# A graph kernel: the GRU state as one operation over both halves, LeakyReLU on ScalarE, and other times in the scheduler's account

## Chip, cores and metric

The kernel runs on one core of a Trainium2 chip. The metric is the device time of one execution in microseconds. The kernel before takes 2144.81 us (median of 3 runs, 2143.91 to 2145.84).

## What is computed

The input is 128 graphs of 128 nodes with 256 features (x), and an adjacency matrix per graph. Two residual layers follow each other, each after a layer norm and a ReLU. All is float32.

```
def _gru_cell(inp, h, w_ih, w_hh, b_ih, b_hh):
    gi = inp @ w_ih.T + b_ih
    gh = h @ w_hh.T + b_hh
    i_r, i_z, i_n = jnp.split(gi, 3, axis=-1)
    h_r, h_z, h_n = jnp.split(gh, 3, axis=-1)
    r = jax.nn.sigmoid(i_r + h_r)
    z = jax.nn.sigmoid(i_z + h_z)
    n = jnp.tanh(i_n + r * h_n)
    return (1.0 - z) * n + z * h
...
for i in range(L):
    m = jnp.einsum('bnd,de->bne', h, weight[i])
    aggr = jnp.einsum('bst,bsd->btd', A, m)
    h = _gru_cell(aggr, h, w_ih, w_hh, b_ih, b_hh)
...
Wh = jnp.einsum('bnf,of->bno', h, W)
s1 = Wh @ a1
s2 = Wh @ a2
e = jax.nn.leaky_relu(s1[:, :, None] + s2[:, None, :], negative_slope=ALPHA)
e = jnp.where(mask, -jnp.inf, e)
att = jax.nn.softmax(e, axis=-1)
att = jnp.where(mask, 0.0, att)
return jnp.einsum('bij,bjo->bio', att, Wh)
```

## The kernel before

**Tiles.** Four graphs make a group (G = 4), so there are 32 groups. The state of a group is held in columns: features on partitions, the 512 nodes of the group on the free axis, in two halves of 128 features (`hT`, 128x2x512). The gathering over neighbours needs it in rows (`h`, nodes on partitions).

**One GRU step** (`gru_step`, from L662) makes the gate products of a group. Two blocks of seven products each follow one another. A product is three matmuls of 128x256, into one of the PSUM banks c1_0, c1_1, c2, u and m7; Strassen-like sums save one product of eight (`moving_sums`, L447; `stationary_sums`). In each block the order is: u, m7, u again, c1_0, u again, c2, c1_1. Bank u is used three times. After its second product VectorE must compute c2 = u + m (L711) before TensorE can go on in u; that addition lies beside the product of c1_0. After its third, ScalarE copies u to c1_1 (L716), and VectorE computes c22 = u + m (L720), before the next block begins in u. ScalarE evaluates the gates (L738, L745, L773). Sigmoids are written as tanh, so factors 0.5 appear.

**Candidate and state.** `candidate` (L625) multiplies the reset gate into the hidden part, one operation for each half (L629). `state` (L633), once for each half, applies Tanh on ScalarE (L637) and then three VectorE operations (L639, L641, L645).

**Between steps.** Before the next step of a group the new state is brought into rows: by TensorE when the next step of the group comes two slots later (`rows`), else by 32x32 block transposes on VectorE and two trips of four DMAs through DRAM (`to_rows_by_blocks`, L537; L546). `prologue` normalises a new group and makes its columns: by TensorE (`to_columns`, L455; L462, copies L472) for the first four groups, by blocks and DRAM (`to_columns_by_blocks`, L514; L523) for later ones.

**Second layer** (`epilogue`, L860). The state goes back to rows; x is loaded again (`load_x1`, two buffers) and added (L886, L884 in the last three groups); then norm, ReLU (L435), two score products per graph (L903), the second score spread over partitions by a DRAM line (in the last three groups by TensorE, L913); then the score sum on ScalarE (L939), LeakyReLU on VectorE (L946), mask (L950, L952), row maximum (L958), Exp (L962), a transpose (L566 and DRAM, or TensorE L971 with the copy L975), the two products pq (L593) and po (L1003), the residual (L1010), and the store.

**What sets the order.** Steps of several groups are interleaved: a plan sorts the steps (g, l) by 3g + 4l, so that the steps of one group lie two to four slots apart. Every instruction is put in program order by a scheduler within the kernel (class `Order`, L171). Side work is written as generators. Each `yield (engine, length, ready, room)` names an engine, a length in us, the time from which it can start, and perhaps a buffer to wait for. `fill` puts such work behind the products, engine by engine, as the reckoned clock has room; an engine named in `close` must be clear again when the product ends. The numbers in the yields are the account; they cost no time on the chip, but they decide the order of each queue. LAND = 2.5 is the account's time for a DMA to land, HOP = 0.2 for a handover. All DMAs are issued from one queue, SP, in this order.

Of the kernel before, what the change touches and what calls it, by code (L numbers as in the profile page):

```python
# [8 lines left out]
F32 = mybir.dt.float32  # L9
# [8 lines left out]
G = 4  # L18
# [9 lines left out]
def preln_gnn_kernel(  # L28
# [30 lines left out]
    def dma(dst, src):  # L59
        put(nc.sync.dma_start(dst, src))  # L60
# [110 lines left out]
    class Order:  # L171
        def __init__(self):
            self.free = dict.fromkeys((PE, ACT, DVE, POOL, SP, "port"), 0.0)
            self.tasks = []

            self.rooms = {"misc": [0.0] * 3, "tq": [0.0] * 2, "h": [0.0] * ROWS, "x1": [0.0] * 2, "prT": [0.0] * 2}
            self.next, self.room_of = dict.fromkeys(self.rooms, 0), {}

        def begin(self, engine, ready, room=None, count=1):
# [20 lines left out]
        def open(self, room, name):  # L200
            self.room_of[name] = room, self.next[room]
            self.next[room] = (self.next[room] + 1) % len(self.rooms[room])
            if room == "misc":
                return ps_misc.tile([P, T], F32, tag="misc", name=name)
            if room == "h":
                return work.tile([P, G, D], F32, tag="h", name=name, bufs=ROWS)
            if room == "prT":
                return work.tile([P, G, P], F32, tag="prT", name=name)
            if room == "x1":
                return io.tile([P, G, D], F32, tag="x1", name=name, bufs=2)  # L210
            return work.tile([P, C, T], F32, tag=room, name=name)
# [214 lines left out]
        put(nc.gpsimd.tensor_tensor(nb[:, all_], nb[:, all_], rstd[:, all_], ALU.mult))  # L426
        return rstd, nb, t

    def norm_apply(src, graphs, rstd, nb, ready, name, h=None):

        for k in graphs:
            t = yield (ACT, 0.5, ready, "h") if h is None else (ACT, 0.5, ready)
            if h is None:
                h = order.open("h", f"h_{name}")
            put(nc.scalar.activation(  # L435
                h[:, k, :], src[:, k, :], AF.Relu, bias=nb[:, k : k + 1], scale=rstd[:, k : k + 1]
            ))
        return h, t
# [183 lines left out]
    def state_rows(s):  # L622
        s.h, s.h_ready = yield from to_rows_by_blocks(s.hT, s.hT_ready, f"{s.g}_{s.l}")

    def candidate(s, r, v, ready):  # L625

        for o in (1, 0):
            s.v_ready[o] = yield DVE2, 0.62, ready[o]
            put(nc.vector.scalar_tensor_tensor(  # L629
                v[:, o, :], r[:, o, :], 1.0, v[:, o, :], ALU.add, ALU.mult  # L630
            ))

    def state(s, o, old, new, v, z, ready):  # L633

        n = v[:, o, :]
        t = yield ACT, 0.66, ready
        put(nc.scalar.activation(n, n, AF.Tanh, bias=bih[:, 2 * C + o : 2 * C + o + 1], scale=1.0))  # L637
        t = yield DVE2, 0.62, t
        put(nc.vector.tensor_tensor(new[:, o, :], old[:, o, :], n, ALU.subtract))  # L639
        t = yield DVE2, 0.62, t - HOP  # L640
        put(nc.vector.scalar_tensor_tensor(  # L641
            new[:, o, :], z[:, o, :], 1.0, new[:, o, :], ALU.add, ALU.mult
        ))
        t = yield DVE2, 0.62, t - HOP
        put(nc.vector.scalar_tensor_tensor(new[:, o, :], new[:, o, :], 0.5, n, ALU.mult, ALU.add))  # L645
        s.halves.append(t)
        if len(s.halves) == C:
            s.hT, s.aT = new, None
            s.l += 1
            if s.l < NL:  # L650
                s.hT_ready = max(s.halves)
                if s.by_blocks():
                    s.rows = order.add(1, state_rows(s))
                if s.due:
                    s.task = order.add(0, inputs(s, s.hT_ready))
            else:

                pairs = range(G // 2)
                for p in [pairs] if s.g < NG - 1 else [pairs[:1], pairs[1:]]:
                    order.add(2, epilogue(s, p, max(s.halves)))  # L660

    def gru_step(s, last):  # L662
# [94 lines left out]
        reset(0, high, c1[1][:, 0, :], done)  # L757
        banks["c1_1"] = state_half(0, high, c1[1][:, 1, :], done)
        t1 = state_half(1, high, c22[:, 1, :], t22)
        s.v_ready = [0.0, 0.0]  # L760
        half_task = order.add(0, candidate(s, r, v, (banks["c1_1"], t1)))


        phase = blocks(1, [(1, (hid, given)), (2, (given,))])
# [11 lines left out]
            return t  # L776

        def add_half(o, cols, src, ready):
            t = order.take(DVE, 0.38, max(ready, s.v_ready[o]))
            put(nc.vector.tensor_tensor(v[:, o, cols], v[:, o, cols], src, ALU.add))  # L780
            return t

# [17 lines left out]
    class Group:  # L800


        def __init__(self, g):
            self.g, self.l, self.entered, self.aT = g, 0, False, None
            (self.xt, _), (self.at, self.at_ready) = xts.pop(g), ats.pop(g)
            self.scales = scales.pop(g)
            self.prT = None
            self.due = False

        def by_blocks(self):  # L810
# [2 lines left out]

    def load_x1(s):

        s.x1_ready = LAND + 1.5 + (yield SP, 0.45, 0.0, "x1")
        s.x1 = order.open("x1", f"x1_{s.g}")
        dma(s.x1, x[s.g * G : (s.g + 1) * G].rearrange("b t d -> t b d"))

# [18 lines left out]
    def prologue(s):  # L838

        g = s.g  # L840
        s.h = None
        parts = s.scales if g == 0 else [s.scales]
        for i, (rstd, nb, t) in enumerate(parts):
            n = G // len(parts)
            graphs = range(i * n, i * n + n)
            s.h, t = yield from norm_apply(s.xt, graphs, rstd, nb, t, f"a{g}", s.h)
        s.h_ready = t
        if g + XT < NG:
            order.add(1, load_task(load_rows, xts, g + XT, t))
        t2 = yield DVE, 0.36, s.at_ready  # L850
        s.A = work.tile([P, G, P], F32, tag="A", name=f"A_{g}", bufs=6)
        put(nc.vector.tensor_scalar(s.A, s.at, 0.0, None, ALU.not_equal))
        if g + AT < NG:
            order.add(1, load_task(load_adjacency, ats, g + AT, t2))
        transposed = to_columns if g < 4 else to_columns_by_blocks
        s.hT, s.hT_ready = yield from transposed(s.h, t, f"a{g}")
        if s.entered:
            s.task = order.add(0, inputs(s, s.hT_ready))

    def epilogue(s, pairs, ready):  # L860

# [6 lines left out]
        bank_t, row_t, graph_t = 0.57 * n / G + 0.02, 0.62 * n / G + 0.02, 0.11 * n  # L868

        late, h = g >= NG - 3, None  # L870
        if late:
            banks, ready = yield from to_rows(s.hT, ready, f"{name}_o", pairs)
        else:
            h, ready = yield from to_rows_by_blocks(s.hT, ready, f"b{name}")
            if g < NG - XT:
                yield from load_x1(s)
                ready = max(ready, s.x1_ready)
# [7 lines left out]
            else:  # L885
                put(nc.vector.tensor_add(x1[:, k2, :], x1[:, k2, :], h[:, k2, :]))  # L886
        rstd, nb, t = yield from norm_scales(x1, graphs, t - HOP, f"b{name}")
        h, t = yield from norm_apply(x1, graphs, rstd, nb, t, f"b{name}", h)

        v = small.tile([P, 2, G], F32, tag="s", name=f"s_{name}")  # L890
        one, two = v[:, 0, :], v[:, 1, :] if late else score_tiles[g % 2][:, 0:G]
# [13 lines left out]
                    accum_out=(one, two)[i][:, k : k + 1],  # L905
                ))

        e = None
        if late:
            t = yield PE, graph_t, t, "misc"  # L910
            p2 = order.open("misc", f"ps2_{name}")
# [4 lines left out]
        else:  # L916
# [5 lines left out]
            for q in range(Q):  # L922
# [2 lines left out]
                    line = dram.tile([G, P], F32, tag="line", name=f"line_{name}")  # L925
                part_q = slice(q * 32, (q + 1) * 32)
                dma(line[:, part_q], turned[q * 32 : q * 32 + G, :])
            t = yield SP, 0.45, t + LAND
            e = work.tile([P, G, P], F32, tag="e", name=f"e_{name}")
            dma(e, line.rearrange("(o k) p -> o k p", o=1).to_broadcast([P, G, P]))  # L930
            t = t + 2.5
            t = t + LAND
        ready = t
        for k in graphs:
            t = yield ACT, 0.4, ready
            if e is None:
                e = work.tile([P, G, P], F32, tag="e", name=f"e_{name}")
            src = p2[:, k * P : (k + 1) * P] if late else e[:, k, :]
            put(nc.scalar.activation(  # L939
                e[:, k, :], src, AF.Identity, bias=one[:, k : k + 1], scale=1.0  # L940
            ))
        if late:
            order.close(f"ps2_{name}", t)
        le = e[:, part, :]
        t = yield DVE2, row_t, t
        put(nc.vector.scalar_tensor_tensor(le, le, ALPHA, le, ALU.mult, ALU.max))  # L946

        off_ready = yield DVE, 0.36 * n / G, ready
        off = s.A[:, part, :]
# [35 lines left out]
        ))  # L985

        banks, ready = yield from gathered(h, prT, t, f"pq_{name}", graphs)
        order.close(f"h_b{name}", ready)
        hs = None
        for c, pq in enumerate(banks):  # L990
            t = yield ACT, bank_t, ready
            order.close(f"pq_{name}_{c}", t)
            if hs is None:
                hs = work.tile([P, C, T], F32, tag="hs", name=f"hs_{name}")
            put(nc.scalar.copy(hs[:, c, cols], pq[:, cols]))
        ready = t
        for half in pairs:
            t = yield PE, 1.73, ready, "misc"
            po = order.open("misc", f"po_{g}_{half}").rearrange("p (k d) -> p k d", d=D)
            for j in range(2):  # L1000
                k = half * 2 + j
                for c in range(C):
                    put(nc.tensor.matmul(  # L1003
                        po[:, j, :], hs[:, c, k * P : (k + 1) * P], gwt[:, c, :],
                        start=(c == 0), stop=(c == C - 1),
                    ))
            for j in range(2):
                k = half * 2 + j
                t2 = yield DVE, 0.4, t
# [5 lines left out]
        ks = slice(g * G + part.start, g * G + part.stop)  # L1015
        dma(out[ks].rearrange("b t d -> t b d"), x1[:, part, :])
        if g < NG - XT:
            order.close(f"x1_{g}", t + LAND)

# [135 lines left out]
```

## Time and profile before

| what | us |
|---|---|
| median of the runs | 2144.81 |
| the profiled execution | 2144.55 |
| its span | 2142.7 |
| TensorE busy | 2118.7 |
| VectorE busy | 1782.2 |
| ScalarE busy | 1295.0 |
| GpSimd busy | 119.1 |
| state operations L639, L641, L645 (VectorE) | 395.6 |
| candidate L629 (VectorE) | 123.4 |
| LeakyReLU L946 (VectorE) | 21.5 |
| score sum L939 (ScalarE) | 41.3 |

The span runs from the first to the last instruction of the profiled execution, and the execution is 1.9 us longer. In the lists, PE is TensorE, PEld its weight loads, DVE is VectorE, ACT ScalarE, POOL GpSimd, and SPq the queue that issues DMAs. A busy time is a sum over the whole span; most of it lies beside other engines' work. A group's line reads: source line, engine, operation, written tile <- read tiles, count, busy time, mean ns of one. A timeline line begins with start and duration; in brackets stands how long the engine had been idle before it, and what ended that. A line of waits reads: who <- for whom: us in total, how many times, the longest. TensorE's float32 matmuls appear as two passes each. Matmuls are pipelined, so that a listed duration is longer than the distance from one to the next.

### The profile page before, as it was taken

The page shows a single profiled execution, that of the slowest core. Times are in us where ns is not written, and L with a number is a line of the kernel's source. Part 1 is how long each engine was busy: PE and PEld are TensorE (multiplying, and loading weights), DVE is VectorE, ACT ScalarE, POOL GpSimd, SP SyncE. Part 2 cuts the span into 40 slices and gives each one's busy share as a digit, 9 for nine tenths or more (in the row PEclk, how much of TensorE's full clock was granted, in tenths as well). Part 3 has the DMA queues.
Part 4 walks back from the last instruction along what each step waited for, and adds up shares of the span by engine and source line. Part 5 has one row for each costly group of instructions (what it writes and reads, how often), then busy time and mean ns, then how long its engine had stood idle before and what let it go on. Part 6 is the DMA issues. An engine that isn't in the chain of part 4 may idle for free.

```text
span 2142.7 us, 32496 instructions
## 1 busy us (share of the span) xinstructions
PE 2118.7 (99%) x10779; PEld 1882.7 (88%) x10779; DVE 1782.2 (83%) x4176; ACT 1295.0 (60%) x2859; POOL 119.1 (6%) x204
## 2 busy tenths in 40 slices
PE   8999999999999999999999999999999999999997
PEld 7888888888888888888888888888888888888886
DVE  7778888888888888888888888888888888888776
ACT  5556656565566666656655565656656566565664
POOL 1000000000000000000000000000000000000000
PEclk9999999999999999999999999999999999999998
DMA  4144353535454255553535545354542544443301
GB/s 138 39 90 89 75 122 84 124 68 130 109 117 115 59 125 109 119 113 73 125 84 127 120 88 124 70 127 105 119 113 64 120 109 109 95 90 82 84 25 40
DMA packets 659240, 209.85 MB, mean 98 GB/s; under 512 B 569856, under 2 KB 636160, under 8 KB 659072
## 3 DMA queue, kind: packets, MB, share of 16 engines
q1 hardware_dynamic: 659072, 207.77, 43.3%
q8 instruction: 85, 1.39, 0.3%
q14 instruction: 83, 0.68, 0.1%
HBM read 120.86 MB, written 86.83 MB: 97 GB/s over the span
## 4 chain that ended last, share of the span: by engine, by line
PE 97%; DVE 2%; DMA 1%; issue 0%; SPq 0%; ACT 0%; DVEq 0%
PE c L685 34%; PE u L685 34%; PE m L685 11%; PE pa L593 8%; PE po L1003 5%; PE pq L593 3%; PE pw L356 1%; DMA x<-in_x 0%; PE pt_a L462 0%; DMA wih<-in_w_ih_t 0%; DVE prT L903 0%; DVE hT L639 0%; DMA out<-x 0%; DVE hT L641 0%; DVE c L711 0%
## 5 line engine op out<-in xcount | busy, mean ns | idle before, releaser
L773 ACT ACTIVATE z<-c,brz 128x256 f32<-128x256 f32 x384 | 185.1, 482 | 303.5 <-PE c L685 139.2
L685 PE MATMUL u<-t_h,s_hh 128*128 128x256 f32 x1152 | 343.0, 379 | 3.8 <-DVE c L711 3.8
L685 PE MATMUL c<-aT,s_f 128*128 128x256 f32 x1152 | 311.3, 379 | 0.0
L685 PE MATMUL u<-t_a,s_f 128*128 128x256 f32 x1152 | 311.3, 379 | 0.0
L738 ACT ACTIVATE r<-c,brz 128x256 f32<-128x256 f32 x384 | 174.3, 477 | 218.3 <-PE c L685 113.8
L780 DVE TENSOR_TENSOR v<-v,c 128x256 f32<-128x256 f32 x384 | 155.1, 418 | 132.1 <-ACT z L773 72.3
L685 PEld LDWEIGHTS u<-t_h,s_hh 128*128 128x128 f32 x1152 | 218.1, 190 | 34.7 <-DVE c L711 5.0
L685 PEld LDWEIGHTS u<-t_a,s_f 128*128 128x128 f32 x1152 | 218.9, 190 | 29.8
L685 PEld LDWEIGHTS c<-aT,s_f 128*128 128x128 f32 x1152 | 218.9, 190 | 29.8
L685 PE MATMUL c<-hT,s_hh 128*128 128x256 f32 x768 | 228.5, 379 | 0.0
L716 ACT COPY c<-u 128x512 f32<-128x512 f32 x192 | 109.5, 570 | 143.2 <-PE u L685 142.5
L711 DVE TENSOR_TENSOR c<-u,m 128x512 f32<-128x512 f32 x192 | 134.2, 699 | 72.4 <-PE u L685 70.4
L708 ACT COPY m<-m 128x512 f32<-128x512 f32 x192 | 112.6, 586 | 101.7 <-PE m L685 99.3
L745 ACT ACTIVATE v<-c,bhn 128x256 f32<-128x256 f32 x384 | 173.1, 481 | 0.0
L720 DVE TENSOR_TENSOR c<-u,m 128x512 f32<-128x512 f32 x192 | 131.5, 685 | 49.2 <-ACT c L716 49.2
L685 PE MATMUL m<-t_h,s_hh 128*128 128x256 f32 x576 | 171.5, 379 | 0.0
L685 PE MATMUL c<-t_h,s_hh 128*128 128x256 f32 x576 | 171.3, 379 | 0.0
L685 PEld LDWEIGHTS c<-hT,s_hh 128*128 128x128 f32 x768 | 144.8, 190 | 19.1
L685 PE MATMUL c<-t_a,s_f 128*128 128x256 f32 x576 | 155.7, 379 | 0.0
L685 PE MATMUL m<-t_a,s_f 128*128 128x256 f32 x576 | 155.6, 379 | 0.0
L685 PE MATMUL u<-aT,s_f 128*128 128x256 f32 x576 | 155.6, 379 | 0.0
L629 DVE SCALAR_TENSOR_TENSOR v<-r,v 128x512 f32<-128x512 f32 x192 | 123.4, 684 | 30.3 <-ACT v L745 28.8
(126 smaller groups left out, 3971.5 us busy)
## 6 DMA issues: line engine op xcount, KB each, us to landing
z<-tq SPq DMA_DIRECT2D x248, 128.0 KB
h<-z SPq DMA_DIRECT2D x248, 128.0 KB
xt<-in_x SPq DMA_DIRECT2D x31, 512.0 KB
z_b<-tq_b SPq DMA_DIRECT2D x116, 128.0 KB
h_b<-z_b SPq DMA_DIRECT2D x116, 128.0 KB
x<-in_x SPq DMA_DIRECT2D x29, 512.0 KB
out<-x SPq DMA_DIRECT2D x29, 512.0 KB
z_a<-tq_a SPq DMA_DIRECT2D x112, 128.0 KB
```

The costliest lines, as they stand in the source:

```text
L593: put(nc.tensor.matmul(pa[:, k * P : (k + 1) * P], h[:, k, c * P : (c + 1) * P], A[:, k, :], start=True, stop=True,))
L629: put(nc.vector.scalar_tensor_tensor(v[:, o, :], r[:, o, :], 1.0, v[:, o, :], ALU.add, ALU.mult))
L685: put(nc.tensor.matmul(to(q), S[0][:, gate_no, weight, :], moving, start=first and q == 0 and i == 0, stop=(i == len(ends) - 1), skip_grou ...
L708: put(nc.scalar.copy(m, m7))
L711: put(nc.vector.tensor_tensor(c2, u, m, ALU.add))
L716: put(nc.scalar.copy(c1[1], u))
L720: put(nc.vector.tensor_tensor(c22, u, m, ALU.add))
L738: put(nc.scalar.activation(r[:, o, cols], src, AF.Tanh, bias=brz[:, o : o + 1], scale=0.5))
L745: put(nc.scalar.activation(v[:, o, cols], src, AF.Identity, bias=bhn[:, o : o + 1], scale=0.5))
L773: put(nc.scalar.activation(z[:, o, cols], src, AF.Tanh, bias=brz[:, C + o : C + o + 1], scale=0.5))
L780: put(nc.vector.tensor_tensor(v[:, o, cols], v[:, o, cols], src, ALU.add))
L1003: put(nc.tensor.matmul(po[:, j, :], hs[:, c, k * P : (k + 1) * P], gwt[:, c, :], start=(c == 0), stop=(c == C - 1),))
```

## The change

- `candidate` and the three operations of `state` work on both halves at once (128x1024 instead of two of 128x512). They start when both halves are there. Their length in the account is 1.22 instead of 0.62.
- LeakyReLU goes from a VectorE operation of its own into the ScalarE activation that adds the first score (Prelu with alpha instead of Identity).
- The account's landing time of the x load of the second layer is 5.0 instead of 4.0, that of its store 4.5 instead of 2.5.
- The buffers of e and hs become rooms of the account. The late groups take tiles of other pools for e, hs and the normalised rows. The two parts of the last group share e, hs and the rows.
- Columns come from TensorE for the first two groups only (g < 2), not the first four.

```diff
-            self.rooms = {"misc": [0.0] * 3, "tq": [0.0] * 2, "h": [0.0] * ROWS, "x1": [0.0] * 2, "prT": [0.0] * 2}
+            self.rooms = {room: [0.0] * 2 for room in ("tq", "x1", "prT", "e", "hs")}
+            self.rooms |= {"misc": [0.0] * 3, "h": [0.0] * ROWS}
...
+    def flat(tile_):
+        return tile_.rearrange("p c t -> p (c t)")
+
     def candidate(s, r, v, ready):
 
-        for o in (1, 0):
-            s.v_ready[o] = yield DVE2, 0.62, ready[o]
-            put(nc.vector.scalar_tensor_tensor(
-                v[:, o, :], r[:, o, :], 1.0, v[:, o, :], ALU.add, ALU.mult
-            ))
+        t = s.v_ready = yield DVE2, 1.22, ready
+        put(nc.vector.scalar_tensor_tensor(flat(v), flat(r), 1.0, flat(v), ALU.add, ALU.mult))
 
     def state(s, o, old, new, v, z, ready):
 
         n = v[:, o, :]
         t = yield ACT, 0.66, ready
         put(nc.scalar.activation(n, n, AF.Tanh, bias=bih[:, 2 * C + o : 2 * C + o + 1], scale=1.0))
-        t = yield DVE2, 0.62, t
-        put(nc.vector.tensor_tensor(new[:, o, :], old[:, o, :], n, ALU.subtract))
-        t = yield DVE2, 0.62, t - HOP
-        put(nc.vector.scalar_tensor_tensor(
-            new[:, o, :], z[:, o, :], 1.0, new[:, o, :], ALU.add, ALU.mult
-        ))
-        t = yield DVE2, 0.62, t - HOP
-        put(nc.vector.scalar_tensor_tensor(new[:, o, :], new[:, o, :], 0.5, n, ALU.mult, ALU.add))
         s.halves.append(t)
         if len(s.halves) == C:
+            n, new_, z_ = flat(v), flat(new), flat(z)
+            t = yield DVE2, 1.22, max(s.halves)
+            put(nc.vector.tensor_tensor(new_, flat(old), n, ALU.subtract))
+            t = yield DVE2, 1.22, t - HOP
+            put(nc.vector.scalar_tensor_tensor(new_, z_, 1.0, new_, ALU.add, ALU.mult))
+            t = yield DVE2, 1.22, t - HOP
+            put(nc.vector.scalar_tensor_tensor(new_, new_, 0.5, n, ALU.mult, ALU.add))
+            s.halves.append(t)
             s.hT, s.aT = new, None
...
-        half_task = order.add(0, candidate(s, r, v, (banks["c1_1"], t1)))
+        half_task = order.add(0, candidate(s, r, v, max(banks["c1_1"], t1)))
...
-        s.x1_ready = LAND + 1.5 + (yield SP, 0.45, 0.0, "x1")
+        s.x1_ready = 5.0 + (yield SP, 0.45, 0.0, "x1")
...
-        transposed = to_columns if g < 4 else to_columns_by_blocks
+        transposed = to_columns if g < 2 else to_columns_by_blocks
...
+        end = g >= NG - 2
+        e_room, hs_room = (None, None) if end else ("e", "hs")
...
-        h, t = yield from norm_apply(x1, graphs, rstd, nb, t, f"b{name}", h)
+        h, t = yield from norm_apply(
+            x1, graphs, rstd, nb, t, f"b{name}", s.kept, "tq" if end else "h"
+        )
...
-            t = yield SP, 0.45, t + LAND
-            e = work.tile([P, G, P], F32, tag="e", name=f"e_{name}")
-            dma(e, line.rearrange("(o k) p -> o k p", o=1).to_broadcast([P, G, P]))
+            t = yield SP, 0.45, t + LAND, "e"
+            s.e = order.open("e", f"e_{g}")
+            dma(s.e, line.rearrange("(o k) p -> o k p", o=1).to_broadcast([P, G, P]))
...
             put(nc.scalar.activation(
-                e[:, k, :], src, AF.Identity, bias=one[:, k : k + 1], scale=1.0
+                e[:, k, :], src, AF.Prelu, bias=one[:, k : k + 1], scale=1.0, alpha=ALPHA
             ))
...
-        t = yield DVE2, row_t, t
-        put(nc.vector.scalar_tensor_tensor(le, le, ALPHA, le, ALU.mult, ALU.max))
...
         if g < NG - XT:
-            order.close(f"x1_{g}", t + LAND)
+            order.close(f"x1_{g}", t + 4.5)
```

More of the change, by code (lines that the diff above doesn't have):

```diff
@@ L206, in open @@
                 return work.tile([P, G, D], F32, tag="h", name=name, bufs=ROWS)
-            if room == "prT":
-                return work.tile([P, G, P], F32, tag="prT", name=name)
+            if room in ("prT", "e"):
+                return work.tile([P, G, P], F32, tag=room, name=name)
             if room == "x1":
@@ L427, in norm_scales, with norm_apply @@
         return rstd, nb, t
-    def norm_apply(src, graphs, rstd, nb, ready, name, h=None):
+    def norm_apply(src, graphs, rstd, nb, ready, name, kept, room="h"):
         for k in graphs:
-            t = yield (ACT, 0.5, ready, "h") if h is None else (ACT, 0.5, ready)
-            if h is None:
-                h = order.open("h", f"h_{name}")
+            t = yield (ACT, 0.5, ready) if kept else (ACT, 0.5, ready, room)
+            if not kept:
+                h = order.open(room, f"h_{name}")
+                if room == "tq":
+                    h = h.rearrange("p c t -> p (c t)").rearrange("p (k d) -> p k d", d=D)
+                kept.append(h)
+            h = kept[0]
             put(nc.scalar.activation(
@@ L759, in gru_step @@
         t1 = state_half(1, high, c22[:, 1, :], t22)
-        s.v_ready = [0.0, 0.0]
-        half_task = order.add(0, candidate(s, r, v, (banks["c1_1"], t1)))
+        s.v_ready = 0.0
+        half_task = order.add(0, candidate(s, r, v, max(banks["c1_1"], t1)))
         phase = blocks(1, [(1, (hid, given)), (2, (given,))])
@@ L778, in add_half @@
         def add_half(o, cols, src, ready):
-            t = order.take(DVE, 0.38, max(ready, s.v_ready[o]))
+            t = order.take(DVE, 0.38, max(ready, s.v_ready))
             put(nc.vector.tensor_tensor(v[:, o, cols], v[:, o, cols], src, ALU.add))
@@ L806, in __init__ @@
             self.scales = scales.pop(g)
-            self.prT = None
+            self.kept, self.prT = [], None
+            self.e = self.hs = None
             self.due = False
@@ L840, in prologue @@
         g = s.g
-        s.h = None
+        kept = []
         parts = s.scales if g == 0 else [s.scales]
@@ L845, in prologue @@
             graphs = range(i * n, i * n + n)
-            s.h, t = yield from norm_apply(s.xt, graphs, rstd, nb, t, f"a{g}", s.h)
+            s.h, t = yield from norm_apply(s.xt, graphs, rstd, nb, t, f"a{g}", kept)
         s.h_ready = t
@@ L858, in prologue, with place_of_e @@
             s.task = order.add(0, inputs(s, s.hT_ready))
+    def place_of_e(g):
+        if g < NG - 2:
+            return order.open("e", f"e_{g}")
+        return work.tile([P, 4, H], F32, tag="th", name=f"e_{g}")[:, 0:2, :].rearrange(
+            "p n t -> p (n t)"
+        ).rearrange("p (k s) -> p k s", s=P)
     def epilogue(s, pairs, ready):
@@ L874, in epilogue @@
             h, ready = yield from to_rows_by_blocks(s.hT, ready, f"b{name}")
+            s.kept.append(h)
             if g < NG - XT:
@@ L906, in epilogue @@
                 ))
-        e = None
         if late:
@@ L934, in epilogue @@
         for k in graphs:
-            t = yield ACT, 0.4, ready
-            if e is None:
-                e = work.tile([P, G, P], F32, tag="e", name=f"e_{name}")
+            t = yield (ACT, 0.4, ready, e_room) if s.e is None else (ACT, 0.4, ready)
+            if s.e is None:
+                s.e = place_of_e(g)
+            e = s.e
             src = p2[:, k * P : (k + 1) * P] if late else e[:, k, :]
             put(nc.scalar.activation(
-                e[:, k, :], src, AF.Identity, bias=one[:, k : k + 1], scale=1.0
+                e[:, k, :], src, AF.Prelu, bias=one[:, k : k + 1], scale=1.0, alpha=ALPHA
             ))
@@ L987, in epilogue @@
         banks, ready = yield from gathered(h, prT, t, f"pq_{name}", graphs)
-        order.close(f"h_b{name}", ready)
-        hs = None
+        final = pairs[-1] + 1 == G // 2
+        if final:
+            order.close(f"h_b{g}_0", ready)
+        if final and not end:
+            order.close(f"e_{g}", ready)
         for c, pq in enumerate(banks):
-            t = yield ACT, bank_t, ready
+            t = yield (ACT, bank_t, ready, hs_room) if s.hs is None else (ACT, bank_t, ready)
             order.close(f"pq_{name}_{c}", t)
-            if hs is None:
-                hs = work.tile([P, C, T], F32, tag="hs", name=f"hs_{name}")
+            if s.hs is None and end:
+                hs = work.tile([P, 4, H], F32, tag="ta", name=f"hs_{g}")
+                s.hs = hs.rearrange("p n t -> p (n t)").rearrange("p (c t) -> p c t", c=C)
+            elif s.hs is None:
+                s.hs = order.open("hs", f"hs_{g}")
+            hs = s.hs
             put(nc.scalar.copy(hs[:, c, cols], pq[:, cols]))
@@ L1006, in epilogue @@
                     ))
+            if final and half == pairs[-1] and not end:
+                order.close(f"hs_{g}", t)
             for j in range(2):
```

## The prediction, made before the changed kernel had run

> **What bounds the kernel now.** I read the page first (busy shares, slices, chain of waits), then the waits of TensorE, the timeline around each, and last the end of the span.
>
> ```profile
> span 2142.7 us, 32496 instructions
> ...
> PE 2118.7 (99%) x10779; PEld 1882.7 (88%) x10779; DVE 1782.2 (83%) x4176; ACT 1295.0 (60%) x2859; POOL 119.1 (6%) x204
> ...
> PE 97%; DVE 2%; DMA 1%; issue 0%; SPq 0%; ACT 0%; DVEq 0%
> ```
>
> TensorE bounds the span. From 6.55 us to the end of its last GRU product at 2103.60 it issues one pass of 128x256 every 0.216 us with hardly a gap. So a shorter VectorE or ScalarE operation is worth nothing in itself. Time can come from four places only: fewer passes, the few places where TensorE waits, the last 36 us, and new waits. The waits of TensorE:
>
> ```profile
> PE ps L913 <- DVE prT L903: 5.6, 1, 5.6
> PE pw L356 <- DMA wih<-in_w_ih_t: 3.9, 1, 3.9
> PE u L685 <- DVE c L711: 3.8, 3, 2.5
> PE pq L593 <- ACT prT L975: 3.3, 3, 2.2
> PE po L1003 <- DVE xt L1010: 1.5, 1, 1.5
> ```
>
> The second is the start and isn't touched. The third is two stalls of 2.50 and 1.04 us at 1821.92 and 1868.30 (0.30 more at 23.72). The others lie behind 2103.60. The larger stall in the timeline:
>
> ```profile
> 1812.42 1.26 SPq L60 DMA_DIRECT2D x<-in_x  x1
> ...
> 1817.31 1.29 DVE L886 TENSOR_TENSOR x<-x,h_b 128x512 f32<-128x512 f32 x2 [2.81 <-DMA x<-in_x]
> ...
> 1821.17 0.69 DVE L711 TENSOR_TENSOR c<-u,m 128x512 f32<-128x512 f32 x1
> ...
> 1821.92 0.70 PE L685 MATMUL u<-t_h,s_hh 128*128 128x256 f32 x2 [2.50 <-DVE c L711]
> ```
>
> The residual add stood in VectorE's queue before its x had landed (4.9 us after the issue; the order reckons 4.0). L711, which frees bank u, stood behind it, and TensorE behind that.
>
> **Part by part.** The profiled execution took 2144.55 us, its span 2142.7; the median of the runs is 2144.81, 0.26 above. I sum against 2144.55.
>
> 1. Columns of groups 2 and 3 through DRAM instead of TensorE (the bound is now g < 2):
>
> ```profile
> 40.30 1.04 PE L462 MATMUL pt_a<-ident,h_a 128*128 128x128 f32 x8
> 41.17 1.03 PE L356 MATMUL pw<-wih,wt 128*128 128x256 f32 x4
> ```
>
> Eight transposes hold the stream from 40.30 to 41.17, 0.87 us; two groups, -1.7. Added: four block transposes on VectorE (0.694 each, L523), 16 DMAs on SP's queue; gone: four copies (0.583) on ScalarE. Cover: group 2 enters in the fourth step, at about 87 us, group 3 at about 150. Counting the matmuls between the block transposes and the first use in the changed order gives over 39 us, against 21.3 in the tightest place where the kernel does this now without a wait. SP's queue has room there: before the first state rows (about 70 us) it holds only loads. Without cover the loss would be some 12 us once. I take 0.
>
> 2. One operation over both halves. L645 takes 691 ns for 512 elements, L780 takes 418 for 256: 1.06 ns an element, so 1024 cost 0.691 + 512 x 0.00106 = 1.23 us. Eight operations of 0.68 to 0.69 a step (5.5 us) become four (4.9): 0.55 x 96 = 53 us less on VectorE, plus LeakyReLU (L946, 20.6 + 0.9), minus 2.8: 1782 to about 1710. Worth on the path: 0, as long as TensorE is fed. What it could cost: L711 has only about 0.4 us of room (released by the product of u, it takes 0.70, and the product of c1 beside it takes 1.30). A 1.23-us operation in front of it can be late by more than one of 0.69. I added up VectorE's work between each two such additions, in both orders, against TensorE's work between them. The tightest interval now is 9.83 us of work in 9.07 of TensorE (isolated durations; followers overlap by about 0.08), it recurs 12 times and stalls nowhere. The tightest in the changed order is 11.28 in 10.85. The order also now reckons 1.22 for what I put at 1.23, where it had 0.62 for 0.69. So 0 to +1 us; I take 0.3. Delay of the state to its second half is covered: its row form is needed three slots (65 us) later.
>
> A rule speaks against longer operations. "SBUF — State Buffer", SBUF: two separate sides, says that a VectorE operation with two SBUF inputs and a GpSimd operation that reads SBUF take one port pair as an exclusive lock for the whole instruction. By it GpSimd's three-step norm could wait 0.54 longer at each step, 1.6 us a norm. The rows do show GpSimd swinging: L422 takes 1192 ns for norm_b and 1036 for norm_a. But ScalarE waited for that norm only 1.6 us (h_a) and 0.8 us (h_b) in the whole steady part, and in the end the norms of the last group fall behind the last wide operation. By rule or row: 0 on the path.
>
> 3. Leaky ReLU inside the first score's activation (ScalarE). No row shows that function; Identity at the same line takes 402 ns (L939), and the built order still has one table load. Bounds: 0 to +0.2 us an instruction; below nothing I exclude, since the instruction count stays. ScalarE is 60% busy; only in the end would this lie on the path, 8 instructions, +1 us at most. I take 0.
>
> 4. Longer times in the order's account, rooms for e and hs. In the two stalls the residual add follows the last L1010 of the group whose buffer it reuses by about 10 us (10.4 and 9.6, counted from the order); elsewhere now 13.2 or more, without a wait. In the changed order the shortest is 19.4. Both stalls go: -3.5. What is next late: the return of e to TensorE (11.5 us after its block transpose against 10.1 now), and the score to its activation (9.0 against 11.2, where the trip line-to-e takes about 5), the rows of one late group (10.1 against 10.8), the transposes of group 30 (0.2 us of room). I put +0.3 for these.
>
> 5. The end. Seen now: from 2103.60 to the end of the last L1010 at 2139.46, 35.9 us, VectorE's chain first, then TensorE's. A wait of 5.57 us there cools TensorE:
>
> ```profile
> 2105.00:2115.00 10.00, 7.28 (x44) 6.06 (x44) 9.31 (x32) 2.86 (x6) 0.00 (x0) 1.00 0.00 0
> 2115.00:2120.00 5.00, 0.00 (x0) 0.00 (x0) 4.78 (x12) 2.47 (x7) 3.07 (x6) 0.76 0.30 105
> 2120.00:2124.00 4.00, 2.76 (x8) 1.49 (x9) 3.65 (x20) 3.50 (x13) 0.00 (x0) 0.50 0.02 6
> ```
>
> (the column before the last two is the clock). In the changed order, from the last GRU product as 0, with the rows' durations: both Tanh end at 2.3; VectorE fills this time with four score products of group 30, then three state operations to 6.15 (now: six, to 4.55, no score product yet); four more score products to 8.4; the residual add of group 31 from 9.2; statistics to 11.35; softmax work of group 30, its LeakyReLU gone, reduce at 14.05; its Exp to 15.7; pq of 30 to 18.25; po to 22.4; pq of the first half of 31 to 24.2; first score of the second half from ScalarE at 25.3; mask, reduce to 26.4; Exp to 27.3; transpose, copy, pq to 29.1; po to 31.55; L1036 to 32.5. That is 3.4 less than 35.9: 0.69 + 0.43 + 0.43 are the LeakyReLUs, the rest is the fill during Tanh and a shorter cold stretch. The four transposes of e for group 29 (0.44) stand behind the last product instead of before it, in time that TensorE waits anyway: another -0.4.
>
> A rule decides 0.8 us of it. "TensorE: Matmul & The Clock Gate", Part 1, gives half rate after an idle window of about 3.4 us. The trace agrees at 5.57 us (0.50; pq takes 3.78 against 1.95 warm) and stays at 1.00 after a gap of 2.16. In the changed order TensorE has only 0.4 us of work in the first 4.6 us. By the rule it is cold and the residual add starts at 9.2, by the row of 2.16 at 8.4. I take the rule's; by the row the end is -4.2.
>
> Sum: -1.7 - 3.5 - 0.4 - 3.4 + 0.3 + 0.3 = -8.4; 2144.55 - 8.4 = 2136.1, and with the 0.26, 2136.4 us, 0.39% faster.
>
> **Rivals.**
> - A wait takes the place of the one removed: one place in the recurring pattern (nine steps, 195 us, some 10 times) where e or a wide operation is late by 0.5 us, 10 x 0.5 = +5, 2141.4. For it: the tight room of L711. Against: every such distance that I counted is as long as one without a wait now, or nearly. 0.14.
> - Slower: wide operations that start just before bank u is released. One costs at most 1.23 - 0.4 = 0.8 us of TensorE. From 16 collisions the whole 12.7 (8.4 to lose, 4.3 to be seen as slower) is gone, so from two places in the recurring pattern: 20 x 0.85 = 17, 2153. Against: the order holds VectorE clear before that addition. 0.04.
> - The loads still come late, since SP's queue was the cause and not the account: 2136.4 + 3.5 = 2139.9. Against: the distances of 19.4 and more. 0.10.
> - The change doesn't do what it says in the end, the serial chain gains nothing: 2136.4 + 3.8 = 2140.2. 0.10, half of it within 0.2%.
> - Forecast case: 0.62, 2133.5 to 2139.
>
> **How the numbers follow.** A measurement of this kernel can tell about 0.2%, 4.3 us, from no change. Faster: 0.62 + 0.10 + 0.05 + some of the first rival's milder forms (0.04) = 0.81; slower 0.04; same 0.15. The range goes down to 2132.5 (a warm end -0.8, both +0.3 at nothing, 2 us of my hand-made end) and up to 2141.5, the first rival.
>
> **What would show it.** Right: no wait of u for L716, the new L711, beyond 0.3 us; pt_a rows x16 instead of x32; the last GRU product ends near 2098; from there to the last L1036 about 32.5 us; wide rows at 1.2 us x96; VectorE near 1710. Wrong: a u wait that recurs about every 195 us; x<-in_x still as a releaser of the residual add; wide operations well over 1.3 us.

## The result, and the profile after

| kernel | median us | against before, 95% interval | span of the profiled execution | its time |
|---|---|---|---|---|
| before | 2144.89 (20 runs beside the other) | 1 | 2142.7 | 2144.55 |
| changed | 2141.83 (2139.42 to 2143.65, 20 runs) | 0.9985 [0.9979, 0.9992] | 2139.5 | 2141.27 |

The change makes the kernel 3.1 us (0.15%) faster. The forecast was 2136.4, so more than half of the expected gain is missing; 2141.83 lies 0.3 above the range, and 0.15% is inside the 0.2% that the forecast took as no change. The first rival, a wait that takes the place of the one removed, stood at 2141.4. One of the 20 runs of the kernel before took 2471.66 us, the others 2143.57 to 2146.26; the median hardly feels it.

The page of the changed kernel says nearly what it said before; no share tells that a gain is missing.

```profile
span 2139.5 us, 32119 instructions
...
PE 2120.0 (99%) x10763; PEld 1881.6 (88%) x10763; DVE 1724.7 (81%) x3763; ACT 1301.8 (61%) x2855; POOL 104.8 (5%) x204
...
PE 96%; DMA 1%; DVE 1%; SPq 1%; ACT 1%; issue 0%; DVEq 0%; ACTq 0%
```

The list of TensorE's waits of the changed kernel tells more (waiting tile <- what it waited for: us in total, times, longest):

```profile
PE pp L988 <- ACT e L979: 3.9, 3, 2.7
PE pw L357 <- DMA wih<-in_w_ih_t: 3.8, 1, 3.8
PE pq L598 <- DMA e<-z_e: 3.1, 3, 1.6
PE pq L598 <- ACT prT L992: 2.3, 4, 0.7
...
PE u L690 <- DVE c L716: 0.3, 1, 0.3
```

The stalls of bank u are down from 3.8 us to the 0.3 at the start. The third line is new: three times in the middle of the stream, pq (the product that reads e) waits for the second leg of e's trip through DRAM: four DMAs write e there (z_e<-prT, the first leg), four bring it back (e<-z_e, the second).

The wide operations and the Prelu cost what the sum reckoned (groups by form of the changed kernel: count, busy us, mean ns, idle time ahead and its releaser):

```profile
L636 DVE SCALAR_TENSOR_TENSOR v<-r,v 128x1024 f32<-128x1024 f32 x96 | 117.4, 1223 | 20.2 <-ACT v L750 18.4
L649 DVE SCALAR_TENSOR_TENSOR hT<-z,hT 128x1024 f32<-128x1024 f32 x96 | 117.0, 1219 | 0.6
...
L958 ACT ACTIVATE e<-e,s 128x128 f32<-128x128 f32 x116 | 39.6, 399 | 0.0
L903 DVE TENSOR_TENSOR x<-x,h_b 128x512 f32<-128x512 f32 x58 | 38.4, 678 | 0.1
```

1.22 us against the 1.23 reckoned; 399 ns against 402 for Identity. The residual add L903 no longer has a load as its releaser. VectorE fell by 57.5 us (the forecast had about 72), of which nothing shows in the time.

**Where the 3.2 us of the two spans come from.** I split each profiled span at the first gate product and at the end of the last one. "Work" is the counted TensorE work in between, each form at the spacing that it has where nothing waits; "lost" is the stream minus this work. About 1.6 remain in streams without any listed wait in their middle (5.41 - 3.84 in before, 1.56 and 1.68 in two runs below). "End" runs from the last gate product to the last residual.

| us | start | stream | work | lost | end |
|---|---|---|---|---|---|
| before | 15.22 | 2088.38 | 2082.97 | 5.41 | 35.86 |
| changed | 14.22 | 2087.41 | 2080.81 | 6.60 | 34.61 |
| difference | -1.00 | -0.97 | -2.16 | +1.19 | -1.25 |

The two stalls account for -3.54 of "lost", so something new took 4.7. A second count finds the same. The changed order repeats itself every nine steps, and e makes three trips in that time. The first of the three starts with its block transpose at 259.75, 456.79, 651.79 and so on up to 1824.11 us; the distances are 197.04, 195.00, 196.50, 194.97, 195.28, 195.08, 195.51, 194.98. The undisturbed distance is 194.97, so the excess is 4.6 us.

### The profile page after: what moved, and what is told of

It reads as the page before. It is cut to its first block, busy times and chain, and to the rows that moved or that the text cites. A ratio compares the mean times of both kernels' runs of the same rounds, so it can differ in the third digit from the quotient of the medians.

```text
span 2139.5 us, 32119 instructions
## 1 busy us (share of the span) xinstructions
PE 2120.0 (99%) x10763; PEld 1881.6 (88%) x10763; DVE 1724.7 (81%) x3763; ACT 1301.8 (61%) x2855; POOL 104.8 (5%) x204
## 4 chain that ended last, share of the span: by engine, by line
PE 96%; DMA 1%; DVE 1%; SPq 1%; ACT 1%; issue 0%; DVEq 0%; ACTq 0%
PE c L690 35%; PE u L690 34%; PE m L690 11%; PE pa L598 8%; PE po L1027 5%; PE pq L598 3%; PE pw L357 1%; SPq L60 1%; DMA z_e<-prT 0%; DMA e<-z_e 0%; DMA wih<-in_w_ih_t 0%; ACT e L979 0%; DVE t_h L458 0%; PE pr_o L489 0%; ACT v L642 0%
## 5 line engine op out<-in xcount | busy, mean ns | idle before, releaser
L716 DVE TENSOR_TENSOR c<-u,m 128x512 f32<-128x512 f32 x192 | 134.1, 698 | 144.5 <-PE u L690 144.4
L721 ACT COPY c<-u 128x512 f32<-128x512 f32 x192 | 109.5, 570 | 117.8 <-PE u L690 117.5
L710 ACT COPY c<-u 128x512 f32<-128x512 f32 x192 | 109.5, 570 | 52.7 <-PE u L690 52.6
```

The lines of the kernel that those rows point to most:

```text
L710: put(nc.scalar.copy(c1[0], u))
L716: put(nc.vector.tensor_tensor(c2, u, m, ALU.add))
L721: put(nc.scalar.copy(c1[1], u))
```

## Why e came late

This is the tightest trip of e in the kernel before (timeline of before; start and duration, then engine, line and tile):

```profile
343.99 0.70 DVE L566 STREAM_TRANSPOSE prT<-e 128x512 f32<-128x512 f32 x1
344.71 2.56 SPq L60 DMA_DIRECT2D z_e<-prT  x4
349.02 1.70 SPq L60 DMA_DIRECT2D e<-z_e  x4
350.76 1.81 SPq L60 DMA_DIRECT2D h<-z  x4
354.76 1.95 PE L593 MATMUL pq<-e,h_b 128*128 128x128 f32 x16
```

SP's queue issues the first leg 0.03 us after the transpose has ended. The next entry, the second leg, stands alone behind it, and the load of the state rows comes after both. pq follows 10.8 us after the transpose began, without a wait. The same trip in the changed kernel, one of eight like it:

```profile
371.66 3.75 SPq L60 DMA_DIRECT2D z<-tq  x4
...
377.27 0.70 DVE L571 STREAM_TRANSPOSE prT<-e 128x512 f32<-128x512 f32 x1
378.93 2.83 SPq L60 DMA_DIRECT2D h<-z  x4
...
381.80 2.80 SPq L60 DMA_DIRECT2D z_e<-prT  x4
384.67 0.60 SPq L60 DMA_DIRECT2D x<-in_x  x1
386.28 1.70 SPq L60 DMA_DIRECT2D e<-z_e  x4
...
390.11 2.02 PE L598 MATMUL pq<-e,h_b 128*128 128x128 f32 x16 [1.64 <-DMA e<-z_e]
```

Here the four loads of state rows stand ahead of the first leg. They can't be issued before their z has landed, 3.5 us after the last issue of z at 375.41 (the account reckons 2.5), and the queue issues in order. So the first leg starts 3.83 us after the transpose instead of 0.03. Then x, 512 KB, goes out between the legs. The second leg takes 2.13 us from its last issue to pq. TensorE was ready for e 11.0 us after the start of the transpose, as in the undisturbed trips, and had it at 12.8.

In the eight trips of this kind the first leg starts 1.5 to 3.8 us late, and pq 12.84, 11.04, 12.49, 11.04, 11.25, 11.04, 11.08 and 11.36 us after the start of the transpose. Against 11.04 that is 3.8 us in all, of the 4.6 in the count by periods. The list of waits shows 3.1: a wait shorter than about 0.16 us, by which the listed durations of pipelined matmuls overlap, leaves no gap.

My theory after this: e's trip is late for what stands in SP's queue ahead of its legs. Two entries are suspected: x between the legs (theory A in the texts below) and the rows h ahead of the first leg (B, later B2). The rivals were wide operations that delay L716, columns or ScalarE as new causes, and the end (C; D is its clock).

## Experiments

Ratios are against the kernel before on the same chip, with the 95% interval. "Lost" and "end" are taken as above from one profiled execution each; two executions of one program differ by over 1 us in span (the changed kernel once more, below).

**The account alone.**

```diff
-        s.x1_ready = LAND + 1.5 + (yield SP, 0.45, 0.0, "x1")
+        s.x1_ready = 5.0 + (yield SP, 0.45, 0.0, "x1")
...
-            order.close(f"x1_{g}", t + LAND)
+            order.close(f"x1_{g}", t + 4.5)
```

These two lines, put into the kernel before. 

> The kernel before with nothing but the longer times of load (5.0) and store (4.5) of x in the account. If they alone take the two stalls away: TensorE's wait of u for VectorE falls from 3.8 to 0.3 us, and the time is 3.5 lower, about 2141.3. If the lighter VectorE was needed: a wait of 1 us or more stays.

Measured: 2141.01, 0.9980 [0.9973, 0.9988]. Lost 1.56 instead of 5.41, end 36.10. Its waits of TensorE:

```profile
PE ps L913 <- DVE prT L903: 5.6, 1, 5.6
...
PE u L685 <- DVE c L711: 0.3, 1, 0.3
```

Two numbers cure both stalls and give as much as the whole change. The end is as before, so nothing else is in it.

**The same two lines taken back in the changed kernel.** 

> The changed kernel with the old times of load (4.0) and store (2.5) of x in the account. If the longer times are what took the two stalls of 2.5 and 1.0 us away: a wait of u for VectorE's addition comes back, 1 us or more in total. If the lighter VectorE or the other pattern did it: no such wait. Theory A says that e's wait depends on where x stands in SP's queue, so that it changes too; time 2138 to 2145.

Measured: 2156.7, 1.0054 [1.0042, 1.0066], slower than before. Here x is issued ahead of the first leg as well. e is late in seven listed places (11.7 us) and u at two (2.3). Without its account the rest of the change costs about 11 us.

**Columns alone** (`g < 4` to `g < 2` in the kernel before). 

> The kernel before with columns from TensorE for two groups instead of four, nothing else. Prediction's part 1: sixteen transposes less, 1.7 us lower (2143.1), no wait for the columns.

Measured: 2144.24, 0.9998 [0.9990, 1.0007]. The work between is 2081.24, 1.73 less than before, as reckoned. But lost is 5.94 and the end 36.18: the stalls of bank u stay (2.7 us), and one for the first sums (L333, 0.8) is new. The time doesn't tell it from before.

**LeakyReLU on ScalarE alone**, in the kernel before:

```diff
-                e[:, k, :], src, AF.Identity, bias=one[:, k : k + 1], scale=1.0
+                e[:, k, :], src, AF.Prelu, bias=one[:, k : k + 1], scale=1.0, alpha=ALPHA
...
-        t = yield DVE2, row_t, t
-        put(nc.vector.scalar_tensor_tensor(le, le, ALPHA, le, ALU.mult, ALU.max))
```

> The kernel before with LeakyReLU in ScalarE's first-score activation and no VectorE operation for it, nothing else. The activation costs as much as before (400 ns). On TensorE's stream 0; in the end up to 1.5 us less (0.69 + 0.43 + 0.43). Its order differs, so the two stalls of 3.5 us may go too: 2140 to 2145.

Measured: 2141.41, 0.9983 [0.9976, 0.9989]. Lost 1.82: with one yield fewer the order is another one, e's trip recurs every 65 us with 12.3 us from transpose to pq, and the stalls are gone though the account of x is the old one. The end falls to 31.26, while the work before it grows to 2088.20. So this gain isn't shown to be the operation's own; it comes with another order.

**The changed kernel with candidate and state on halves again.** 

> The changed kernel with candidate and state on halves again. If wide operations cost TensorE nothing, as its trace suggests (0.3 us of wait behind VectorE's addition), the time in the steady part is the same but for e's place in SP's queue, which is another here (12.1 us to e's return instead of 11.5): e's wait goes, 2138 to 2141. If the wide operations are what made the pattern longer and the change slow: 3 us or more lower than the changed kernel, with no wait for e.

Measured: 2140.95, 0.9980 [0.9972, 0.9988]. Lost 3.50, end 32.02, no wait for e (0.8 us of what is lost is a wait for the first sums; the work before the end grows to 2086.47 in this order). The trip has the 65-us pattern of the LeakyReLU run, h is ahead of the first leg by 1.0 to 2.3 us here too, but TensorE comes 12.3 us after the transpose. So without the wide operations the kernel isn't slower, and the tight nine-step pattern comes with them. Why the scheduler falls into it isn't shown; the wide operations alone in the kernel before were not tried.

**x behind e's second leg**, in the changed kernel (`order.close(f"x1_{g}", t + 4.5)` becomes `t + 11.5`; only SP's order differs). 

> The changed kernel; the only difference is that in the recurring pattern the load of x for the second layer stands behind the four DMAs that bring e back, not between the two legs of e's trip (the account's time for the store of x is 11.5 instead of 4.5; the order of TensorE, VectorE, ScalarE and GpSimd is the same). Theory A (e comes back late because its second leg waits in SP's queue behind the x load, at a place that recurs every 195 us): TensorE's wait for e (3.1 us in the changed kernel's trace) goes below 0.5, and the time is about 2138.5 (3 less than 2141.8). Rival B (e is late because the queue is held up ahead of the first leg, by the rows h that wait for their z): the wait stays at 1 to 3 us and the time within 1 us of 2141.8. Rival C (the missing 5 us are all in the end of the span): no change.

Measured: 2140.57, 0.9975 [0.9967, 0.9984]. The second leg now takes 1.75 us from its last issue to pq instead of 2.13. The waits for e fall from 3.1 to 1.6 (0.96 and 0.67 at the two worst places), lost from 6.60 (6.88 in a second execution of the changed kernel) to 5.18. By the traces the order of TensorE, VectorE, ScalarE and GpSimd is the changed kernel's from the first instruction to the last, so the fall comes from x's place in SP's queue. It is a part of the cause and not the whole.

**h behind the first leg.** The account's landing time of z for state rows becomes 7.5, so that the loads of rows are planned later:

```diff
-        ready = t + LAND
+        ready = t + (7.5 if n > G and name[0] not in 'ab' else LAND)
```

> The changed kernel with 7.5 instead of 2.5 us in the account for the landing of z of the state rows, so that at the recurring place e's first leg stands ahead of the rows h in SP's queue; x still stands between e's legs. TensorE, VectorE, ScalarE and GpSimd keep nearly the same order. Theory B2: e's first leg is issued 2 us sooner, TensorE's wait for e is below 0.5 us, time 3 us or more below the changed kernel on the same chip, spread below 3. Theory A (x between the legs is the cause): the wait stays at 2 us or more.

Measured: 2143.9, 0.9995 [0.9987, 1.0003]. The first leg starts 0.02 to 0.03 us after the transpose in all eight places, and the listed waits for e fall to 0.7. But h and x now stand between the legs, pq still comes 11.04 to 11.57 us after the transpose, and lost is 5.08. A u wait of 0.8 at 1821.27 and an end of 35.50 are other parts of the new order. With one of the two entries moved, 1.5 us less is lost than in the changed kernel, but the time doesn't fall: the end is 0.9 longer, though 2.2 us of TensorE's work has moved from it into the stream.

**Both.** The last two edits together. 

> As the run before, with x behind e's second leg too. Theory B2: no wait for e, time as the run before or up to 0.5 us lower, about 0.9965 of the kernel before. Theory A: 2 us lower than the run before.

Measured: 2140.02, 0.9977 [0.9967, 0.9986]; lost 1.68. The same place of the pattern:

```profile
378.01 0.70 DVE L571 STREAM_TRANSPOSE prT<-e 128x512 f32<-128x512 f32 x1
378.75 3.79 SPq L60 DMA_DIRECT2D z_e<-prT  x4
...
382.72 2.05 SPq L60 DMA_DIRECT2D h<-z  x4
384.97 1.80 SPq L60 DMA_DIRECT2D e<-z_e  x4
386.81 0.42 SPq L60 DMA_DIRECT2D x<-in_x  x1
...
389.06 1.95 PE L598 MATMUL pq<-e,h_b 128*128 128x128 f32 x16
```

pq comes 11.04 us after the transpose in all eight, without a wait, and the periods are 194.96 to 194.98 throughout. The whole new loss is gone with the wide operations still in place: it was the queue. The traces leave little else: from 127 to 1882 us TensorE, VectorE, ScalarE and GpSimd have the same instructions in the same order here as in the changed kernel, and this run has them all in the order of the run before, which lost 3.4 more. Neither theory holds alone: it is 3.9 us faster than that run, where B2 allowed 0.5 and A 2. Its end is 35.03 in this order (the last group's first transposes wait 6.9 us for Exp), which takes back 3 against an end of 32.

**A longer account for e's trip** (4.5 instead of 2.5 for its second leg). 

> The changed kernel with 4.5 instead of 2.5 us in the account for the second leg of e's trip through DRAM, so that the product pq of the steady groups is placed about 1.3 us or more behind where it stands. Theory A and rival B: both say that TensorE's wait for e goes (below 0.5 us), last GRU product about 3.5 us earlier than 2101.6, time about 2138.5. Rival C: last GRU product stays near 2101.6.

Measured: 2145.73, 1.0002 [0.9994, 1.0010]. A new order in which e is late again, at another recurring place (six listed waits, 5.2 us; lost 9.25). There rows, columns and store stand ahead of the first leg, which starts 5.0 to 6.0 us after the transpose. A longer time for the trip itself says nothing about what is ahead of it.

**The changed kernel once more.** 

> The changed kernel once more, beside the next three on one chip. Theory B2 (the queue is held up ahead of the first leg of e's trip, by the rows h that wait for their z; how late e is differs from execution to execution): waits for e of 2 to 5 us in the trace, at the places that recur every 195 us, and a spread of the times of 3 us or more. Time about 0.9985 of the kernel before.

Measured: 2142.35, 0.9986 [0.9980, 0.9993]. In its profiled execution e is late in four listed places (2.9 us), 5.1 us by periods; lost is 6.88, the end 32.01. Its 21 runs spread over 8.7 us (2138.04 to 2146.77); the ten of the run with both edits, on the same chip, over 1.3.

**Idle matmuls in the end**: six after the last product, two ahead of pp and one ahead of pq in the last groups (they add work that the reference lacks). In the changed kernel: 

> The changed kernel with idle matmuls (identity times a weight, into a bank that nothing reads) in the gaps of the end: six behind the last GRU product, two ahead of each transpose of e of the last two groups, one ahead of each pq of the late groups. They add work that the reference does not have. Theory D (the end is 2.1 us longer than I reckoned because TensorE ran at half clock twice): pq takes 1.95 instead of 3.78 and 3.68, from the last GRU product to the last residual 31 to 32.5 instead of 34.6, time 2 to 3.5 lower. Rival: the end is set by VectorE and ScalarE, the clock is hidden: less than 0.7 lower, or higher by the added matmuls.

Measured: 2141.9, 0.9980 [0.9971, 0.9989]. The end is 32.10, against 34.61 and 32.01 without them. Since the end also reached 32.0 without them, no gain is shown. In the kernel with both edits to SP's queue: 

> As the run before, with the idle matmuls in the end. Theories B2 and D together: no wait for e, from the last GRU product to the last residual 32 us, 2 to 2.5 us below the run before, about 0.9955 of the kernel before. If the clock of the end is hidden: as the run before.

Measured: 2142.25, 0.9987 [0.9980, 0.9993], end 36.05. They run at once after the last product, and then TensorE waits 6.2 us for Exp (6.9 without them). They miss their purpose there.

## The prediction, step by step

- **Columns, -1.7, and the transposes of group 29, -0.4: right.** The counted work fell by 2.16; columns alone by 1.73.
- **The two stalls, -3.5: right**, cause included: -3.54, and two numbers in the account suffice.
- **Wide operations, +0.3: right as a cost beside L716**, whose wait is 0.3 as before, at 1.22 us each. The port rule that the prediction weighed shows in the rows and cost nothing on the path. A step of GpSimd's norm that takes 0.23 us alone, L425, takes 1.25 us where it starts under a wide operation, and ends 0.08 us behind it (timeline of the changed kernel):

```profile
2024.20 1.23 DVE L636 SCALAR_TENSOR_TENSOR v<-r,v 128x1024 f32<-128x1024 f32 x1 [1.10 <-ACT v L750]
...
2024.26 1.25 POOL L425 TENSOR_SCALAR norm_b<-mv_b 128x4 f32<-128x4 f32 x1
```

In eight places of the pattern it takes 0.65 us and ends 0.09 us behind a wide operation; in the kernel before, the same step took up to 0.66 under the short ones. GpSimd's busy time fell all the same, from 119.1 to 104.8 us. But wide operations came with the pattern in which e is late.
- **Prelu, 0: right** as an operation.
- **"The return of e to TensorE (11.5 us after its block transpose against 10.1 now)", in the +0.3 of what is next late: this step failed.** It measured +4.6 to +4.7. The last GRU product ended at 2101.62, not near 2098. I compared two distances in TensorE's work, found the new one longer, and took the trip as equal. But in the trips that repeat through the kernel before, the first leg leaves 0.03 us after the transpose, and in every third one of the changed order 1.5 to 3.8 us after it, with x between the legs. The distance grew by 0.3 us and not by the 1.4 that I counted (from the end of the transpose 10.1 before and 10.3 in the changed kernel's undisturbed trips, where I had 11.5; from its start 10.8 and 11.0), the trip by more: in its worst place it ended 1.8 us after TensorE was ready. This is the first rival's price, and its mechanism as far as "e is late" (10 places of 0.5 us; seen eight, from 0 to 1.8), for which I gave 0.14 because "every such distance that I counted is as long as one without a wait now, or nearly". What I gave for it, the tight room of L711, had no part in it; that the result lies so near its 2141.4 is partly luck, since the end and the start moved too.
- **The end, 32.5: mis-sized for one execution.** It took 34.61 in the profiled execution, and 32.01 and 32.63 in those of the same kernel and of the run with x moved. Its cold start came as forecast: pq of group 29 took 3.78 us, with a granted clock of 0.50 from 2106 to 2111 (3.42 and 0.66 in the second execution), and the residual add began 9.7 us after the last product (8.7 in the second), where the forecast had 9.2 by the rule of the clock and 8.4 by the row. Of the 2.6 us between these two executions, 1.0 was gone when pq of group 30 began; the other 1.6 lie in this pq, which I had put warm. The timeline of the changed kernel, then that of its second run:

```profile
2119.00 3.68 PE L598 MATMUL pq<-prT,h_b 128*128 128x128 f32 x16 [0.68 <-ACT prT L992]
```

```profile
2119.42 2.05 PE L598 MATMUL pq<-prT,h_b 128*128 128x128 f32 x16 [0.68 <-ACT prT L992]
```

The same sixteen matmuls after the same wait cost 1.6 more in one execution; the granted clock there is 0.69 against 1.00 (2120 to 2124).

In the profiled execution's sum: -2.2 (work), -3.5 (stalls), +4.7 (e), -1.25 (end, -3.4 expected), -1.0 (start, which varies from 14.05 to 15.75 between executions and isn't the change's), together -3.2. Against the forecast of -8.4, e's trip is 4.4 of the 5.2 us that are missing here, and the end 2.2; wide operations (0.3) and the start (1.0) go the other way.

**What stays open.** Why z_e took 3.0 to 3.6 us to land at the one place near 775 us, and 1.7 nearly everywhere else; the remaining 0.8 us of the 4.6; why the wide operations bring the nine-step order; and whether one order can have the whole stream of the run with both edits and the end of 32. Two kernels have medians more than 1 us below the changed one's (x moved, and both edits to SP's queue), but the intervals overlap with its own, so neither is shown to beat it; both beat the kernel before. The case for both edits is the stronger: on one chip its ten runs all lie at or below 2140.76, and 15 of the changed kernel's 21 above.

## What to carry to other kernels

A distance in work is no slack until it is set against the queue that the transfer goes through: list, for each recurring trip, what stands ahead of each of its issues, and whether one of these must itself wait for a landing. After a change of the order, look at each trip's lag from producer to first issue before its distance to the consumer. Where a kernel is bound by one engine, shorter work on another is worth nothing by itself, and a re-planned order can cost more than the change gives; try the account's numbers alone first.

## What the runs showed of the hardware

The clock fell at shorter waits than I had expected. In the run with the old account, pq took 3.65 us after a wait of 2.04 in the middle of the stream (timeline of that run):

```profile
1049.19 3.65 PE L598 MATMUL pq<-e,h_b 128*128 128x128 f32 x16 [2.04 <-DMA e<-z_e]
```

The granted clock was 0.51 from 1049.2 to 1051. After a wait of 2.36 in the same run it took 3.68; after waits of 1.88 and less it took 2.02. But the kernel before stayed at clock 1.00 after gaps of 2.16 in its end and of 2.50 in the middle of the stream (the larger stall of bank u). So the same length of wait can go either way, and the idle window of about 3.4 us, which the prediction took from the Trainium skill ("TensorE: Matmul & The Clock Gate", Part 1), isn't the least that can cost the clock here: the measurement decides. Ahead of the cold pq in the end of the changed kernel, too, no wait was longer than 2.69 us. The same holds for the two executions of the changed kernel: one fell to 0.69 at 2120 after two waits of 0.7 us around four transposes, the other stayed at 1.00 there, though its TensorE was no busier from 2115 to 2120 (3.01 against 3.44 us).
